# Macaron transformer, attention stage: 256 of 8192 exponentials a channel by a polynomial on VectorE, and q and k of a head on two row blocks

## The chip, the cores and the metric

The kernel runs on one core of one Trainium2 chip. The metric is the device time of one launch in microseconds. The kernel before took 8821.56 us in the median of three runs (8819.5 to 8832.62).

## What is computed

Six layers follow each other on x of shape (4, 1024, 128): a mixture of experts, a state-space layer, the mixture again, a second mixture of experts, an attention, and that mixture again. Each is added to x, most after a layernorm. The change lies in the attention alone, which has 16 heads of 8 columns, and 16 "channels" a head. Cut to what matters:

```
Q, K, V = proj(layernorm(x))                     # (4, 16, 1024, 8)
for wl in range(16):                             # channels
    m = cos(phase_modulators)[wl]                # one number a head
    scores = (Q*m) @ (K*m).T / sqrt(8)
    scores = scores * cos(KERR * scores * scores)   # KERR = 2.7e-12
    acc += softmax(scores) @ V * interference_weights[wl]
out = (acc / 16) @ Wo + bo
```

The kernel takes the inner cosine for 1 when a bound on the scores allows it (both branches are in the program; this input takes the short one, `attention_small`). A channel then differs from another only by the factor cc[h, wl] = m*m/sqrt(8) in front of the same 1024 x 1024 scores.

## The kernel before

**Data.** All of x stays in SBUF. A unit u is one head of one batch, 64 in all. `xs[u]` holds its scores transposed (keys on partitions: 128 x 8 x 1024 fp32, less each query's maximum), two buffers. For each of 16 channels ScalarE makes `p_w = exp(cc * xs)` in one instruction of 8192 columns (L812, two buffers), and TensorE multiplies it by `vt` (the head's 8 value columns and a column of ones, which gives the softmax's sum) into `o`: 32 matmuls of 256 columns (L821), in four column blocks (r = 0 to 3), which the profile counts as 64[...]. VectorE copies `o` to `os` (L829), TensorE transposes it (L842), and every second channel VectorE copies the result into `ot` (L846). After 16 channels `weigh` (L753 to L775) divides by the sums, applies the channels' weights and adds the channels up into `comb`.

**Beside that.** `prepare(u)` makes the scores of a later unit in 16 steps: `maxima` (L721), eight steps that score 128 queries against all keys (two matmuls in `score`, L707, counted as four) and reduce them on VectorE (L726), and, at its end, write the negated maxima by matmul and copy into row 0 of the head's block of `qp` (L734, L741); and `head` (L746), eight steps that score with the maxima in place and copy into `xs` (L750). `group` (L685) projects q and k of HG = 4 heads at a time, each head on its own 32 rows of the 128; `batch` (L647) does a batch's layernorm, transposes and values; `out` (L777) projects a finished batch and adds it to x.

**Order.** TensorE and VectorE run in the written order (manual_schedule, L794). Channel by channel it is: matmuls of `o`; copy `os`; at channel 0, `weigh` of the unit before; pieces of group, batch or out in their channels; one step of `prepare` (channel 15 begins the unit after next); the transposes; at odd channels the copy into `ot`. Each engine takes its queue in order, so an instruction that waits holds up all behind it. ScalarE has only the exponentials: that of channel g+2 writes the `p_w` buffer that the matmuls of channel g read.

Of the kernel before, what the change touches and what calls it, by code (L numbers as in the profile page):

```python
# [26 lines left out]
P = 128  # L27
# [16 lines left out]
PI2_1 = 6.28125  # L44
PI2_2 = 0.0019350051879882812
PI2_3 = 2.0 * math.pi - PI2_1 - PI2_2
RSQRT = 1597463007.0
LN_TINY = -87.33654

# [468 lines left out]
    nc.vector.tensor_tensor(xt, xt, k.bo, op=ALU.add)  # L518


HG = 4
NG = H // HG
QQ = 4
QW = L // QQ


def attention(tc, k):
# [8 lines left out]
    with ExitStack() as ctx:  # L536
# [5 lines left out]
        with (  # L542
            tc.tile_pool(name="at_p", bufs=2) as sb,
            tc.tile_pool(name="at_tr", bufs=2, space=PSUM) as ps_tr,
        ):
            z = half_sine(nc, sb, k.pm, H * WL)
            m = sb.tile([P, H * WL], F32, name="m")
            nc.vector.scalar_tensor_tensor(m, z, -2.0, z, op0=ALU.mult, op1=ALU.mult)
            nc.vector.tensor_scalar(m, m, 1.0, None, op0=ALU.add)
            m_hw = m.rearrange("p (w h) -> p h w", h=H)  # L550
            nc.vector.scalar_tensor_tensor(cc, m_hw, SCALE, m_hw, op0=ALU.mult, op1=ALU.mult)
            nc.vector.tensor_scalar(iw, k.iw, 1.0 / WL, None, op0=ALU.mult)

            pb = ps_tr.tile([1, 2, P], F32, name="pb", tag="tr")
            for j, (w_t, b_t) in enumerate(((k.wq, k.bq), (k.wk, k.bk))):
                w2 = sb.tile([C, C], F32, name="w2")
                nc.vector.tensor_tensor(w2, w_t, w_t, op=ALU.mult)
                pn = ps_tr.tile([P, 1], F32, name="pn", tag="pn")  # L560
                nc.tensor.matmul(pn, w2, k.ones[:, 0:1], start=True, stop=True)
                big = sb.tile([P, 1], F32, name="big")
                nc.scalar.activation(big, pn, AF.Sqrt, scale=1.02 * C)
                ab = sb.tile([P, 1], F32, name="ab")
                nc.vector.scalar_tensor_tensor(
                    ab, b_t, -1.0, b_t, op0=ALU.mult, op1=ALU.max
                )
                nc.vector.tensor_tensor(big, big, ab, op=ALU.add)
                nc.tensor.transpose(pb[:, j, :], big, k.ident)
            both = sb.tile([1, 2], F32, name="both")  # L570
            nc.vector.tensor_reduce(both, pb, AX.X, ALU.max)
            bound = sb.tile([1, 1], F32, name="bound")
            nc.vector.scalar_tensor_tensor(
                bound, both[:, 0:1], SCALE * D, both[:, 1:2], op0=ALU.mult, op1=ALU.mult
            )
            nc.vector.scalar_tensor_tensor(
                bound, bound, KERR, bound, op0=ALU.mult, op1=ALU.mult
            )
            nc.vector.tensor_scalar(bound, bound, 1e-4, None, op0=ALU.is_lt)
            nc.vector.tensor_copy(flag, bound)  # L580
# [13 lines left out]
def attention_small(tc, k, cc, iw):  # L594
# [10 lines left out]
    with (  # L605
# [5 lines left out]
        tc.tile_pool(name="as_o", bufs=1, space=PSUM) as ps_o,  # L611
    ):

        wp, bp = [], []
        for x, w_t in (("q", k.wq), ("k", k.wk)):
            w = one.tile([C, NG, HG, 32], F32, name=f"wp_{x}")
            nc.gpsimd.memset(w, 0.0)
            nc.gpsimd.tensor_copy(
                w[:, :, :, 1 : 1 + D], w_t.rearrange("c (g j d) -> c g j d", j=HG, d=D)
            )  # L620
            wp.append(w)
            b_t = one.tile([P, NG], F32, name=f"bp_{x}")
            nc.gpsimd.memset(b_t, 0.0)
            if x == "k":
                for j in range(HG):
                    nc.gpsimd.memset(b_t[32 * j : 32 * j + 1, :], 1.0)
            for j in range(HG):
                nc.sync.dma_start(
                    out=b_t[32 * j + 1 : 32 * j + 1 + D, :],
                    in_=k.b_dram[x].rearrange("(g j d) -> j d g", j=HG, d=D)[j],  # L630
                )
            bp.append(b_t)
        nm = one.tile([P, GT], F32, name="nm")
        vts = []
        for j in range(2):
            vt = one.tile([P, GT, H, D + 1], F32, name=f"vt{j}")
            nc.gpsimd.memset(vt[:, :, :, D : D + 1], 1.0)
            vts.append(vt)
        ob = []
        for j in range(2):  # L640
            o = ps_o.tile([P, 512], F32, name=f"o{j}", tag=f"o{j}")
            nc.vector.memset(o[:, 0:QW], 0.0)
            ob.append(o)

        xnt, qp, kp, comb, xs = {}, {}, {}, {}, {}

        def batch(b):  # L647

# [5 lines left out]
            for half in range(2):  # L654
                pt = ps_t.tile([P, 4, P], F32, name="pt", tag="tr")
                for i in range(4):
                    t = b * GT + half * 4 + i
                    xn = sb.tile([P, C], F32, name="ln_xn", bufs=4)
                    nc.vector.tensor_scalar(
                        xn,  # L660
                        k.x_sb[:, t, :],
# [23 lines left out]
        def group(n):  # L685

            for w, b_t, x, at in zip(wp, bp, "qk", (qp, kp)):
                at[n] = sb.tile([P, L], F32, name=f"{x}p")
                for half in range(2):
                    pq = ps_t.tile([P, 512], F32, name="pq", tag="tr")  # L690
                    nc.tensor.matmul(
                        pq,
                        w[:, n % NG].rearrange("c j d -> c (j d)"),
                        xnt[n // NG][:, ts(half, 512)],
                        start=True,
                        stop=True,
# [9 lines left out]

        def score(j, a, i, c):  # L707

            row = slice(32 * j, 32 * j + 32)
            s = ps_s.tile([P, L], F32, name="s")  # L710
            for half in range(2):
                nc.tensor.matmul(  # L712
                    s[:, ts(half, 512)],
                    a[row, ts(i, P)],
                    c[row, ts(half, 512)],
                    start=True,
                    stop=True,
                )
            return s

        def maxima(u):  # L721

            n, j = divmod(u, HG)
            row = slice(32 * j, 32 * j + 1)
            for i in range(GT):
                nc.vector.tensor_reduce(  # L726
                    nm[:, i : i + 1], score(j, qp[n], i, kp[n]), AX.X, ALU.max, negate=True
                )
                if i < GT - 1:
                    yield  # L730
            for half in range(2):
                pt = ps_t.tile([P, 4, P], F32, name="pt", tag="tr")
                for i in range(4):
                    nc.tensor.matmul(  # L734
                        pt[row, i, :],
                        nm[:, half * 4 + i : half * 4 + i + 1],
                        k.ident,
                        start=True,
                        stop=True,
                    )  # L740
                nc.vector.tensor_copy(  # L741
                    qp[n][row, ts(half, 512)], pt[row].rearrange("p a b -> p (a b)")
                )
            yield

        def head(u):  # L746
            n, j = divmod(u, HG)
            xs[u] = xp.tile([P, GT, L], F32, name="xs")
            for i in range(GT):
                nc.vector.tensor_copy(xs[u][:, i, :], score(j, kp[n], i, qp[n]))  # L750
                yield

        def weigh(u, ot):  # L753

# [11 lines left out]
            )  # L766

            if h == 0:
                comb[b] = sb.tile([P, 2, QQ, C], F32, name="comb")
            nc.vector.tensor_reduce(  # L770
                comb[b].rearrange("p c r e -> p (c r) e")[:, :, ts(h, D)],
                ot[:, :, :, 0:D].rearrange("p w t d -> p t d w"),
# [21 lines left out]
        with tc.manual_schedule(engines={mybir.EngineType.PE, mybir.EngineType.DVE}):  # L794
            finish(batch(0), group(0), prepare(0))
            ahead = prepare(1)
            next(ahead)
            for u in range(n_heads):
                n, j = divmod(u, HG)
                b, h = divmod(u, H)  # L800

                beside = []
                if j == 2 and n + 1 < B * NG:
                    beside.append((10, 14, group(n + 1)))
                if n % NG == 3 and j == 1 and b + 1 < B:
                    beside.append((4, 9, batch(b + 1)))
                if b > 0 and h == 2:
                    beside.append((2, 10, out(b - 1)))
                ot = sb.tile([P, WL, 2 * QQ, D + 1], F32, name="ot", bufs=1)
                for wl in range(WL):  # L810
                    p_w = xp.tile([P, GT, L], F32, name="p_w")
                    nc.scalar.activation(  # L812
                        p_w.rearrange("p a b -> p (a b)"),
                        xs[u].rearrange("p a b -> p (a b)"),
                        AF.Exp,
                        scale=cc[:, h, wl : wl + 1],
                    )
                    o = ob[wl % 2]
                    for i in range(GT):
                        for r in range(QQ):  # L820
                            nc.tensor.matmul(  # L821
                                o[32 * r : 32 * r + D + 1, 0:QW],
                                vts[b % 2][:, i, h, :],
                                p_w[:, i, ts(r, QW)],
                                start=(i == 0),
                                stop=(i == GT - 1),
                            )
# [7 lines left out]
                    if wl == WL - 1 and u + 2 < n_heads:  # L835
                        finish(ahead)
                        ahead = prepare(u + 2)
                    next(ahead, None)
                    if wl % 2 == 0:
                        pt = ps_t.tile([P, 4, P], F32, name="pt", tag="tr")  # L840
                    for c in range(2):
# [152 lines left out]
def load_attention(nc, pool, k, a):  # L994
# [4 lines left out]
    for x in "vo":  # L999
        get(f"w{x}", [C, C], a[f"L1_attn_W{x}"])  # L1000
        get(f"b{x}", [P, C], a[f"L1_attn_b{x}"].partition_broadcast(P))
    k.b_dram = {x: a[f"L1_attn_b{x}"] for x in "qk"}
    get(
        "pm",
        [P, WL * H],
        a["L1_attn_phase_modulators"].rearrange("w h -> (w h)").partition_broadcast(P),
    )
    get("iw", [P, WL], a["L1_attn_interference_weights"].partition_broadcast(P))


# [93 lines left out]
```

## Time and profile before

| | |
|---|---|
| median of three runs | 8821.56 us |
| the profiled execution | 8833.98 us, span 8832.1 us |
| TensorE busy | 7823.0 us (89%) |
| ScalarE busy | 7665.0 us (87%) |
| VectorE busy | 3262.1 us (37%) |
| GpSimd busy | 608.7 us (7%), nearly all before 1300 us |
| mean granted TensorE clock | 0.918 |
| first exponential of L812 starts | 1424.5 us |
| last exponential of L812 starts | 8654.4 us |

A row of the costliest groups reads: line, engine, operation, tiles written and read, shapes, count, then busy us and mean ns of one, then idle time of the engine just before, and what ended most of it. A row of the timeline reads: start, duration, engine, line, operation, tiles, count; in brackets the engine's idle time before it and who ended it. Busy time on TensorE is modelled from overlapping matmuls, so 89% is not 89% of its peak, and its clock (PEclk) is granted between half and full.

### The profile page before, as it was taken

The page shows a single profiled execution, that of the slowest core. Times are in us where ns is not written, and L with a number is a line of the kernel's source. Part 1 is how long each engine was busy: PE and PEld are TensorE (multiplying, and loading weights), DVE is VectorE, ACT ScalarE, POOL GpSimd, SP SyncE. Part 2 cuts the span into 40 slices and gives each one's busy share as a digit, 9 for nine tenths or more (in the row PEclk, how much of TensorE's full clock was granted, in tenths as well). Part 3 has the DMA queues.
Part 4 walks back from the last instruction along what each step waited for, and adds up shares of the span by engine and source line. Part 5 has one row for each costly group of instructions (what it writes and reads, how often), then busy time and mean ns, then how long its engine had stood idle before and what let it go on. Part 6 is the DMA issues. An engine that isn't in the chain of part 4 may idle for free. (4 is left out here: it accounts for less than half of the span.)

```text
span 8832.1 us, 164134 instructions
## 1 busy us (share of the span) xinstructions
PE 7823.0 (89%) x76474; PEld 3392.0 (38%) x76474; DVE 3262.1 (37%) x5409; ACT 7665.0 (87%) x1746; POOL 608.7 (7%) x579
## 2 busy tenths in 40 slices
PE   8888887999899998989999999999999999899985
PEld 5222253333333333333333333333333333333333
DVE  6777773323333333323233323223333333323222
ACT  3333325999999999999999999999999999999992
POOL 3444430000000000000000000000000000000000
PEclk9777787999999999999999999999999999999996
DMA  0000000000000000000000000000000000000000
GB/s 18 0 0 0 0 6 4 1 1 1 1 1 1 1 1 1 1 1 1 1 1 1 1 1 1 1 1 1 1 1 1 1 1 1 1 1 1 1 1 16
DMA packets 14326, 19.40 MB, mean 2 GB/s; under 512 B 2986, under 2 KB 12722, under 8 KB 13620
## 3 DMA queue, kind: packets, MB, share of 16 engines
q8 instruction: 609, 9.98, 0.5%
q1 hardware_dynamic: 9316, 6.01, 0.2%
q10 hardware_dynamic: 4304, 2.62, 0.1%
q14 instruction: 97, 0.79, 0.0%
HBM read 6.53 MB, written 2.10 MB: 1 GB/s over the span
## 5 line engine op out<-in xcount | busy, mean ns | idle before, releaser
L812 ACT ACTIVATE p_w<-xs,cc 128x8192 f32<-128x8192 f32 x1024 | 7188.6, 7109 | 48.5 <-DVE xs L750 29.1
L821 PE MATMUL o<-p_w,vt 128*9 128x256 f32 x65536 | 4055.1, 403 | 654.3 <-ACT p_w L812 653.4
L821 PEld LDWEIGHTS o<-p_w,vt 128*9 128x9 f32 x65536 | 1809.4, 95 | 2608.2 <-ACT p_w L812 804.3
L829 DVE COPY os<-o 128x256 f32<-128x256 f32 x1024 | 434.9, 425 | 3595.2 <-PE o L821 3595.2
L712 PE MATMUL s<-kp,qp 32*128 32x512 f32 x2048 | 1026.5, 621 | 0.0
L712 PE MATMUL s<-qp,kp 32*128 32x512 f32 x2048 | 1022.1, 619 | 0.0
L750 DVE COPY xs<-s 128x1024 f32<-128x1024 f32 x512 | 627.1, 1225 | 730.4 <-PE s L712 724.3
L726 DVE TENSOR_REDUCE nm<-s 128x1 f32<-128x1024 f32 x512 | 626.2, 1223 | 647.5 <-PE s L712 647.5
L712 PEld LDWEIGHTS s<-qp,kp 32*128 32x128 f32 x2048 | 343.6, 186 | 491.2 <-issue 486.9
L712 PEld LDWEIGHTS s<-kp,qp 32*128 32x128 f32 x2048 | 344.7, 186 | 471.7 <-issue 467.0
L842 PEld LDWEIGHTS pt<-ident,os 128*128 128x128 f32 x2048 | 206.2, 141 | 764.1 <-issue 669.0
L354 PE MATMUL yp<-hm,ident 128*128 128x512 f32 x512 | 388.7, 880 | 99.2 <-POOL hm L353 97.7
L842 PE MATMUL pt<-ident,os 128*128 128x128 f32 x2048 | 450.3, 302 | 19.6 <-DVE os L829 9.6
L336 ACT ACTIVATE da<-delta,neg_a 128x512 f32<-128x512 f32 x256 | 182.7, 721 | 291.9 <-DVE hst L342 291.5
L353 POOL TENSOR_TENSOR hm<-hst,c_sb 128x512 f32<-128x512 f32 x256 | 369.9, 1457 | 166.3 <-ACT c_sb L333 113.3
L178 ACT ACTIVATE r<-hp 128x512 f32<-128x512 f32 x160 | 95.5, 597 | 207.9 <-PE hp L176 185.5
L354 PEld LDWEIGHTS yp<-hm,ident 128*128 128x128 f32 x512 | 110.0, 252 | 348.9 <-POOL hm L353 318.0
L340 DVE TENSOR_TENSOR db<-du,bp 128x512 f32<-128x512 f32 x256 | 164.2, 682 | 152.9 <-PE bp L329 152.0
L333 ACT COPY c_sb<-cp 128x512 f32<-128x512 f32 x128 | 74.8, 585 | 166.1 <-PE cp L331 129.0
L342 DVE TENSOR_TENSOR_SCAN hst<-da,last,db 128x512 f32<-128x512 f32 x128 | 192.0, 1540 | 0.0
L180 POOL TENSOR_TENSOR h<-r 128x512 f32<-128x512 f32 x160 | 164.6, 1047 | 201.7 <-ACT r L178 201.3
L342 DVE TENSOR_TENSOR_SCAN hst<-da,db 128x512 f32<-128x512 f32 x128 | 171.1, 1372 | 5.6 <-POOL hm L353 4.4
(176 smaller groups left out, 3102.8 us busy)
## 6 DMA issues: line engine op xcount, KB each, us to landing
x_sb<-in_L_attn_x_dram ACTq DMA_DIRECT2D x4, 512.0 KB
c_w<-in_L_ffn_w_dram SPq DMA_DIRECT2D x4, 512.0 KB
out_dram<-x_sb SPq DMA_DIRECT2D x4, 512.0 KB
c_w<-in_L_ffn_w_stack_dram SPq DMA_DIRECT2D x1, 512.0 KB
c_w<-in_L_ffn_w_stack_dram ACTq DMA_DIRECT2D x1, 512.0 KB
c_ws<-in_L_ffn_ws_dram SPq DMA_DIRECT2D x2, 128.0 KB
c_w_in<-in_L_attn_W_in_dram SPq DMA_DIRECT2D x1, 256.0 KB
c_w_out<-in_L_attn_W_out_dram SPq DMA_DIRECT2D x1, 128.0 KB
```

Source lines behind the costliest of these rows:

```text
L180: nc.gpsimd.tensor_tensor(h, r, r, op=ALU.mult)
L336: nc.scalar.activation(da, delta[:, c, hc], AF.Exp, scale=neg_a[:, c, n : n + 1])
L342: nc.vector.tensor_tensor_scan(hst, da, db, 0.0 if half == 0 else last[:, c, n : n + 1], op0=ALU.mult, op1=ALU.add,)
L353: nc.gpsimd.tensor_tensor(hm, hst, c_sb, op=ALU.mult)
L354: nc.tensor.matmul(yp[c], k.ident, hm, start=(n == 0), stop=(n == NS - 1))
L712: nc.tensor.matmul(s[:, ts(half, 512)], a[row, ts(i, P)], c[row, ts(half, 512)], start=True, stop=True,)
L726: nc.vector.tensor_reduce(nm[:, i : i + 1], score(j, qp[n], i, kp[n]), AX.X, ALU.max, negate=True)
L750: nc.vector.tensor_copy(xs[u][:, i, :], score(j, kp[n], i, qp[n]))
L812: nc.scalar.activation(p_w.rearrange("p a b -> p (a b)"), xs[u].rearrange("p a b -> p (a b)"), AF.Exp, scale=cc[:, h, wl : wl + 1],)
L821: nc.tensor.matmul(o[32 * r : 32 * r + D + 1, 0:QW], vts[b % 2][:, i, h, :], p_w[:, i, ts(r, QW)], start=(i == 0), stop=(i == GT - 1),)
L829: nc.vector.tensor_copy(os, o[:, 0:QW])
L842: nc.tensor.transpose(pt[:, wl % 2 * 2 + c, :], os[:, ts(c, P)], k.ident)
```

## The change

The first 256 of the 8192 columns of each channel's `p_w` are no longer made by ScalarE. VectorE makes them in nine operations: `split` multiplies by cc/ln 2, rounds to an integer p, forms 2^p by shifting into the exponent (as an integer), and takes the rest r; `power` evaluates a polynomial of degree five in r, short of its leading factor. The factor, EXP2_TOP, is put on the values instead: `vtop`, formed once a head, takes the place of `vt` in the one of 32 matmuls that reads these columns. In VectorE's order, channel g carries `split` of g+3 and `power` of g+2, after the step of `prepare` and ahead of the copy into `ot`; `vtop` stands ahead of the head's channel 0.

A group is 2 heads instead of 4. Each head has its q and k twice, on two blocks of 32 rows; `score` takes its first 512 keys from one block and the other 512 from the other. The maxima go to both blocks, by matmuls of 64 columns and an addition. `group` runs once every two heads, at channels 10 to 13, and forms its padded weights each time on GpSimd; `out` begins at channel 1 of the batch's first head (channel 2 of its third before). `ln_xn` has one buffer instead of four in `batch`, `comb` one instead of two, and the mask `pm` is loaded inside the attention.

```diff
-HG = 4
+HG = 2
+SOFT = 256
...
+        def split(g):
+            u, wl = divmod(g, WL)
+            s, c = xs[u][:, 0, 0:SOFT], cc2[:, u % H, wl : wl + 1]
+            r = sb.tile([P, SOFT], F32, name="x_r")
+            nc.vector.tensor_scalar(r, s, c, -127.0, op0=ALU.mult, op1=ALU.max)
+            p = sb.tile([P, SOFT], F32, name="x_p")
+            nc.vector.tensor_scalar(p, r, ROUND, ROUND, op0=ALU.add, op1=ALU.subtract)
+            e = sb.tile([P, SOFT], I32, name="x_e")
+            nc.vector.tensor_scalar(
+                e, p, float(1 << 23), 127.0 * (1 << 23), op0=ALU.mult, op1=ALU.add
+            )
+            nc.vector.tensor_tensor(r, r, p, op=ALU.subtract)
+            return e, r, p
+
+        def power(g, e, r, p):
+            p_w[g] = xp.tile([P, GT, L], F32, name="p_w")
+            nc.vector.scalar_tensor_tensor(p, r, EXP2[4], r, op0=ALU.add, op1=ALU.mult)
+            for c in EXP2[3], EXP2[2], EXP2[1]:
+                nc.vector.scalar_tensor_tensor(p, p, c, r, op0=ALU.add, op1=ALU.mult)
+            nc.vector.scalar_tensor_tensor(
+                p_w[g][:, 0, 0:SOFT], p, EXP2[0], e.bitcast(F32), op0=ALU.add, op1=ALU.mult
+            )
...
         def score(j, a, i, c):
-            row = slice(32 * j, 32 * j + 32)
             s = ps_s.tile([P, L], F32, name="s")
             for half in range(2):
+                row = slice(64 * j + 32 * half, 64 * j + 32 * half + 32)
                 nc.tensor.matmul(
...
+            nc.vector.tensor_copy(nm[:, :, 32], nm[:, :, 0])
...
-                    xn = sb.tile([P, C], F32, name="ln_xn", bufs=4)
+                    xn = sb.tile([P, C], F32, name="ln_xn", bufs=1)
...
+            power(0, *split(0))
+            power(1, *split(1))
+            parts = split(2)
             for u in range(n_heads):
...
+                vtop = sb.tile([P, D + 1], F32, name="vtop")
+                nc.vector.tensor_scalar(vtop, vts[b % 2][:, 0, h], EXP2_TOP, None, op0=ALU.mult)
                 for wl in range(WL):
-                    p_w = xp.tile([P, GT, L], F32, name="p_w")
+                    g = u * WL + wl
                     nc.scalar.activation(
-                        p_w.rearrange("p a b -> p (a b)"),
-                        xs[u].rearrange("p a b -> p (a b)"),
+                        p_w[g].rearrange("p a b -> p (a b)")[:, SOFT:],
+                        xs[u].rearrange("p a b -> p (a b)")[:, SOFT:],
                         AF.Exp,
                         scale=cc[:, h, wl : wl + 1],
                     )
                     o = ob[wl % 2]
                     for i in range(GT):
                         for r in range(QQ):
+                            soft = i * L + r * QW < SOFT
                             nc.tensor.matmul(
                                 o[32 * r : 32 * r + D + 1, 0:QW],
-                                vts[b % 2][:, i, h, :],
-                                p_w[:, i, ts(r, QW)],
+                                vtop if soft else vts[b % 2][:, i, h, :],
+                                p_w[g][:, i, ts(r, QW)],
...
                     next(ahead, None)
+                    done, parts = parts, split(g + 3) if g + 3 < n_heads * WL else None
+                    if done:
+                        power(g + 2, *done)
```

`vtop` is L860 in the changed kernel.

## The prediction

> **What bounds the kernel now.** I read the page's costliest groups first, then who the exponential waits for, then the timeline of single channels. In the groups, ScalarE's exponential of L812 stands alone:
>
> ```profile
> L812 ACT ACTIVATE p_w<-xs,cc 128x8192 f32<-128x8192 f32 x1024 | 7188.6, 7109 | 48.5 <-DVE xs L750 29.1
> ```
>
> and its tile's view says what its idle time (us, times) ended with:
>
> ```profile
>   DVE xs L750: 29.1, 24
>   PE o L821: 19.0, 10
> ```
>
> 7188.6/1024 = 7.02 us from start to start, and 48.5 us of idle in all. Attention is a ScalarE queue without gaps, so the change can win only by shortening L812, and loses by whatever makes it wait. L812 of channel g+2 needs the TensorE product `o` of channel g (two `p_w` buffers). So look at how late `o` may come, and at what speed TensorE runs it:
>
> ```profile
> 4103.74 5.33 PE L821 MATMUL o<-p_w,vt 128*9 128x256 f32 x64 [0.92 <-ACT p_w L812]
> 4109.00 1.98 PE L712 MATMUL s<-qp,kp 32*128 32x512 f32 x4
> 4109.13 0.42 DVE L829 COPY os<-o 128x256 f32<-128x256 f32 x1 [5.21 <-PE o L821]
> 4110.91 0.44 PE L842 MATMUL pt<-ident,os 128*128 128x128 f32 x2
> 4111.01 1.23 DVE L750 COPY xs<-s 128x1024 f32<-128x1024 f32 x1 [1.46 <-PE s L712]
> ...
> 6630.18 3.64 PE L821 MATMUL o<-p_w,vt 128*9 128x256 f32 x64
> 6638.41 6.06 PE L821 MATMUL o<-p_w,vt 128*9 128x256 f32 x64 [2.31 <-ACT p_w L812]
> ```
>
> The same 64 matmuls take 3.64, 5.33 or 6.06 us. The difference is the granted clock, in the windows around the second and the last:
>
> ```profile
> 4103.74:4107.15 3.41, 3.41 (x36) 1.49 (x40) 0.18 (x1) 3.41 (x1) 0.00 (x0) 0.51 0.03 5
> 6634.80:6638.20 3.40, 1.30 (x5) 0.30 (x3) 1.44 (x2) 3.40 (x1) 0.00 (x0) 0.75 0.00 0
> 6638.20:6641.60 3.40, 3.19 (x32) 1.23 (x36) 0.00 (x0) 3.40 (x2) 0.00 (x0) 0.50 0.00 0
> ```
>
> (columns: us, busy PE, PEld, DVE, ACT, POOL, then PEclk). After a stretch with little `o`, TensorE runs at half clock for 3.4 us, or 6.8. Today this is harmless: exp of g+2 comes due 6.9 us after `o` of g may start.
>
> **The change, part by part.** T = end of an exponential.
>
> *Removed from ScalarE:* 256 of 8192 columns. L336 takes 721 ns for 512 columns, L812 7109 for 8192: (7109-721)/7680 = 0.832 ns a column, 0.213 us a channel, x1024 = **-218 us**. Exponentials then come every 6.80 us.
>
> *Added to VectorE, nine 128x256 operations a channel.* The nearest rows are those of half_sine, same shape, each waiting for the one before:
>
> ```profile
> 1347.93 0.29 DVE L474 TENSOR_SCALAR cs_k<-cs_k 128x256 f32<-128x256 f32 x1
> 1348.26 0.43 DVE L476 SCALAR_TENSOR_TENSOR cs_r<-cs_k,c_pm 128x256 f32<-128x256 f32 x1
> 1348.72 0.42 DVE L477 SCALAR_TENSOR_TENSOR cs_r<-cs_k,cs_r 128x256 f32<-128x256 f32 x1
> ```
>
> Start to start, a dependent tensor_scalar costs 0.33, a dependent scalar_tensor_tensor 0.46; an operation that waits for nothing starts 0.085 before the end of the one before (L103: 0.34 long, 0.257 apart). In order: 0.40 (a per-channel scalar adds 0.07: L268 753 ns, L313 682), 0.33, 0.21, 0.34, four times 0.46, 0.34 = **3.46 us**. In an ordinary channel VectorE copies `os` at T+3.7, reduces or copies scores from T+4.8 to 6.0, does the nine until 9.4, copies `ot` until 9.7; its next `os` comes at 6.8+3.7 = 10.5. It keeps up, with 0.8 us over. Cost there: 0.
>
> *Scores on two row blocks.* Four matmuls one after another take 1.98 us now. Where two heads' blocks meet, the trace has
>
> ```profile
> 1419.79 1.21 PE L712 MATMUL s<-kp,qp 32*128 32x512 f32 x1
> 1419.98 1.05 PE L712 MATMUL s<-qp,kp 32*128 32x512 f32 x1
> 1420.80 1.06 PE L712 MATMUL s<-kp,qp 32*128 32x512 f32 x1
> 1420.83 1.05 PE L712 MATMUL s<-qp,kp 32*128 32x512 f32 x1
> ```
>
> Matmuls of different blocks overlap, and the later head's first even starts ahead of the earlier head's last two. The Trainium skill (TensorE: Matmul & The Clock Gate, Part 3, The mechanism) says that matmuls keep program order. By that rule the pairs 1, 2 of one half and 3, 4 of the other overlap only in the middle: 1.5 us. By the rows the halves run side by side: 1.05 us. I take the rows. The wait of exp(head, 0) for L750 (29.1 us) then goes: **-29**. By the rule it goes too; the 0.45 us would come back below.
>
> *The stall at each head's start.* `vtop` (L860) is formed on VectorE at the head's start, behind everything of channel 15: nine operations and the `ot` copy. It ends at T+9.8 (T = end of exp 15), and TensorE's first matmul of channel 0 waits for it, with all of `o` queued behind. `o(0)` could have started at T+6.85; it starts at T+9.85, after about 4.8 idle us. At full clock it would end at 13.4, and exp(2) is due at 13.5 (6.8+6.8-0.1): nothing lost. But the clock: the nearest row is the 6.06 us after 2.31 idle us, 2.4 us more than 3.64. Bounds: 0 if the clock held, 1.7 for one half-clock window, 3.0 for most of two. The Trainium skill (same page, Part 1: The HAM clock gate) lets the clock fall after a whole idle window of about 3.4 us on a fixed grid; 4.8 idle us hold one in (4.8-3.4)/3.4 = 0.4 of the heads, the 4 us below in 0.2. By the row above a window with 1.30 us of TensorE work was enough, so every head pays. I take the row, 2.4: `o(0)` ends at 15.8, exp(2) starts at 15.95, **2.45 us late**.
>
> Then the weighing (L757 to L770, 4037.66 to 4042.22 = 4.56 us) follows `os(0)`, as before, but now with the nine behind it: `os(1)` starts 0.34+4.56+1.14+3.46 = 9.5 us after `os(0)`, at 25.4, ends at 25.8. TensorE's transposes of channel 1 wait for it, and `o(2)` behind them; TensorE is again idle for some 4 us. Transposes at half clock 0.74, `o(2)` starts at 26.6, takes 3.57+2.4, ends at 32.6. Exp(4) is due at 15.95+13.6 = 29.55: **3.15 us late** (at full clock 0.35, bounds 0.35 and 3.75). Sum 5.6 us x 63 heads = **+353** (bounds 22 and 428; by the skill's rule 63 x (0.35+0.6x2.4) = 113).
>
> *Batches and outputs.* Layernorm through one `ln_xn` buffer: each of eight transposes now makes a round trip (0.34+0.05+0.25+0.2 = 0.85 instead of 0.26 us). With statistics (1352.62 to 1358.08: 5.5 us) some 19 us of VectorE work fall on five channels with about 1.1 us over each; the lead of `o` absorbs 3. I take 10 to 20, say 15, three times; the output projections, now beside the weighing, some 7, three times; today's 19.0 us of waits for `o` are in it: **+46** (20 to 80).
>
> *At nothing:* 16 more groups (4 projections of 1.05 us, 4 copies of 0.75) fall on channels with TensorE at 5.1 of 6.8 us; GpSimd's weight copies (L618: 0.3 us) run on an idle engine and wait only for the group before; `maxima` waits for one more 0.16 us copy. Without that cover they cost up to 16 x 4 x 0.75 = 48 us. The exponential's new wait is for the polynomial of two channels earlier, which `o` of that channel waited for anyway. The mask load moves behind one DMA: 0 to 0.5 us; SP's bias loads follow it.
>
> *Start.* The first head's 16 score steps stand 3.41 us apart at half clock, limited by four matmuls; side by side about 1.9. Saved 25, less 3 for the first polynomials: **-22** (-30 to +5).
>
> Sum: -218-29+353+46-22 = **+130**. The profiled execution took 8833.98 (span 8832.1): 8964. It stands 12 above the median of 8821.56, so I forecast 8821.56+130 = about **8950** for the median.
>
> **Rivals.**
> 1. *The clock holds at the head's start*, or TensorE's idle stretch counts as work. Then the stalls are 22 us: -218-29+22+46-22 = -201, 8620; by the skill's idle window 113, so -110, 8710. For it: at full clock both `o` come almost in time, and most gaps in attention don't trip the clock (some 830 of 1024 `o` in the trace run at 3.6). Against: every stretch as empty as this did. One half-clock window (1.7) each time would give 63 x 3.85 = 243, +20, 8842. It turns faster where an `o` after the gap loses less than 1.6 us. Faster by over 0.2%: 0.14.
> 2. *VectorE's chain is longer*: scores in program order (+0.45) or not side by side (+0.9), or dearer operations. Each 0.45 delays both `o`: 63 x 0.9 = +57; serial scores +113, and the 29 return: 9005 to 9095. 0.22.
> 3. *The exponential doesn't shorten* (its cost not per column): 9170. L336 speaks against: 0.02.
>
> **How the numbers follow.** 0.56 for the forecast (8860 to 9000), 0.22 and 0.02 for the slower ones, 0.14 faster, 0.06 within 0.2% (17.6 us, about what a measurement tells from no change). The range 8820 to 9090 leaves out rival 1's full form, rival 3 and a piece of each side.
>
> **What would show it.** L812 at 6.9 us each with idle near 450 us, its releaser `o`, late at channels 2 and 4 of each head; `o` groups of 5 to 6.5 us at channels 0 and 2; PEld of `o` waiting for `vtop`; the nine operations at 0.29 to 0.43 us; score groups near 1.1 us. Wrong if `o(0)` runs in 3.6 us after the wait, or if VectorE reaches `vtop` before T+7.

## The result and the profile after

The changed kernel took 8931.86 us in the median of four runs (8924.35 to 8940.69), beside 8826.35 (8819.5 to 8832.62) for the kernel before, which had one run more than in the table above: 1.012 times as long, 95% interval 1.0103 to 1.0138. The profiled executions stand 90.4 us apart: 8833.98 before, 8924.35 after.

The row of the exponential on the page of the changed kernel, and two rows of the polynomial:

```profile
L863 ACT ACTIVATE p_w<-xs,cc 128x7936 f32<-128x7936 f32 x1024 | 6979.1, 6898 | 372.5 <-PE o L873 230.6
L789 DVE SCALAR_TENSOR_TENSOR x_p<-x_p,x_r 128x256 f32<-128x256 f32 x3072 | 1306.1, 425 | 105.3
L776 DVE TENSOR_SCALAR x_p<-x_r 128x256 f32<-128x256 f32 x1024 | 301.4, 294 | 35.0
```

ScalarE works 209.5 us less than before and waits 324.0 us longer. Its tile's view lists what the waits end with (us, times):

```profile
  PE o L873: 230.6, 76
  issue: 141.9, 63
```

63 of the waits are put down to "issue", that is, to nothing the profile shows. They are channel 2's. The timeline of head 23 shows what they wait for (T, the end of the last exponential of the head before, is 4049.62):

```profile
4059.05 0.30 DVE L901 COPY ot<-pt 128x144 f32<-128x144 f32 x1
4059.27 0.16 DVE L860 TENSOR_SCALAR vtop<-vt 128x9 f32<-128x9 f32 x1
...
4059.48 0.60 PE L873 MATMUL o<-p_w,vtop 128*9 128x256 f32 x1 [4.75 <-DVE vtop L860]
...
4059.88 5.59 PE L873 MATMUL o<-p_w,vt 128*9 128x256 f32 x59
...
4065.60 13.71 ACT L863 ACTIVATE p_w<-xs,cc 128x7936 f32<-128x7936 f32 x2 [2.38 <-issue]
...
4075.11 0.42 DVE L881 COPY os<-o 128x256 f32<-128x256 f32 x1
...
4075.58 0.69 PE L897 MATMUL pt<-ident,os 128*128 128x128 f32 x2 [4.05 <-DVE os L881]
...
4076.59 5.77 PE L873 MATMUL o<-p_w,vt 128*9 128x256 f32 x59
...
4082.49 6.92 ACT L863 ACTIVATE p_w<-xs,cc 128x7936 f32<-128x7936 f32 x1 [3.18 <-PE o L873]
```

Read downwards: VectorE gets to `vtop` only after channel 15's last copy; TensorE, idle for 4.75 us, then needs 6.0 us for `o(0)`; exp(2) starts 0.13 us after `o(0)` has ended, whatever the bracket says. Then `os(1)` is late, TensorE is idle for 4.05 us, `o(2)` takes 6.2 us, and exp(4) waits. The granted clock during `o(0)` (columns as in the prediction; the column after POOL is PEclk):

```profile
4057.47:4060.89 3.42, 1.41 (x16) 0.61 (x20) 1.79 (x6) 3.42 (x1) 0.00 (x0) 0.50 0.00 0
4060.89:4064.30 3.41, 3.41 (x40) 1.28 (x32) 0.00 (x0) 2.33 (x1) 0.00 (x0) 0.50 0.02 5
4064.30:4067.71 3.41, 3.41 (x48) 1.27 (x41) 2.09 (x4) 2.11 (x1) 0.00 (x0) 1.00 0.00 0
```

Where the time went, from the start-to-start distances of L863 in the trace (median 6.801 us; 7.013 before), as excess over the median:

| us | before | after |
|---|---|---|
| 1023 distances at the median | 7174 | 6957 |
| excess at channel 2 | within 0.5 | 147.7 (all heads but the last) |
| excess at channel 4 | within 0.5 | 175.1 (all heads but the first) |
| excess at all other channels | 55.6 | 64.5 |
| first exponential starts | 1424.5 | 1407.9 |
| from the end of the last one to the end of the span | 170.5 | 162.9 |

-217 + 323 + 9 - 17 - 8 = +90, the difference of the two spans. (323 is channels 2 and 4 together.)

### The profile page after: what moved, and what is told of

The parts are those of the page before. It is cut to its first block, busy times and chain, and to the rows that moved or that the text cites. A ratio compares the mean times of both kernels' runs of the same rounds, so it can differ in the third digit from the quotient of the medians.

```text
span 8922.5 us, 174023 instructions
## 1 busy us (share of the span) xinstructions
PE 7329.0 (82%) x76602; PEld 3158.3 (35%) x76602; DVE 6585.9 (74%) x14818; ACT 7455.7 (84%) x1746; POOL 622.5 (7%) x642
## 5 line engine op out<-in xcount | busy, mean ns | idle before, releaser
L863 ACT ACTIVATE p_w<-xs,cc 128x7936 f32<-128x7936 f32 x1024 | 6979.1, 6898 | 372.5 <-PE o L873 230.6
L789 DVE SCALAR_TENSOR_TENSOR x_p<-x_p,x_r 128x256 f32<-128x256 f32 x3072 | 1306.1, 425 | 105.3
L873 PE MATMUL o<-p_w,vtop 128*9 128x256 f32 x2048 | 671.7, 412 | 307.5 <-DVE vtop L860 307.5
L729 PE MATMUL s<-kp,qp 32*128 32x512 f32 x2048 | 588.5, 651 | 0.7 <-DVE nm L743 0.7
L729 PE MATMUL s<-qp,kp 32*128 32x512 f32 x2048 | 583.1, 646 | 0.0
L790 DVE SCALAR_TENSOR_TENSOR p_w<-x_p,x_e 128x256 f32<-128x256 f32 x1024 | 435.6, 425 | 109.4 <-DVE x_p L789 3.7
L787 DVE SCALAR_TENSOR_TENSOR x_p<-x_r 128x256 f32<-128x256 f32 x1024 | 428.3, 418 | 0.1
L781 DVE TENSOR_TENSOR x_r<-x_r,x_p 128x256 f32<-128x256 f32 x1024 | 428.2, 418 | 0.0
L774 DVE TENSOR_SCALAR x_r<-xs,cc 128x256 f32<-128x256 f32 x1024 | 352.8, 345 | 1.0
L776 DVE TENSOR_SCALAR x_p<-x_r 128x256 f32<-128x256 f32 x1024 | 301.4, 294 | 35.0
```

The source lines that it names most:

```text
L729: nc.tensor.matmul(s[:, ts(half, 512)], a[row, ts(i, P)], c[row, ts(half, 512)], start=True, stop=True,)
L781: nc.vector.tensor_tensor(r, r, p, op=ALU.subtract)
L787: nc.vector.scalar_tensor_tensor(p, r, EXP2[4], r, op0=ALU.add, op1=ALU.mult)
L789: nc.vector.scalar_tensor_tensor(p, p, c, r, op0=ALU.add, op1=ALU.mult)
L790: nc.vector.scalar_tensor_tensor(p_w[g][:, 0, 0:SOFT], p, EXP2[0], e.bitcast(F32), op0=ALU.add, op1=ALU.mult,)
L863: nc.scalar.activation(p_w[g].rearrange("p a b -> p (a b)")[:, SOFT:], xs[u].rearrange("p a b -> p (a b)")[:, SOFT:], AF.Exp, scale=cc[:, ...
```

## The experiments

The theory: `vtop`'s place in VectorE's queue empties TensorE, TensorE's clock halves, and the late `o` holds the exponential; the weighing with nine more operations behind it does it again two channels on. The rivals: the weighing does its part alone; VectorE is overfull around a head's start; the clock has nothing to do with it. All kernels below are edits of the changed one, and the ratios, with their 95% intervals, are to the kernel before, which took 8826.07 to 8827.66 us beside them, so that times of different runs can be compared. "Excess" is that of the table above.

**vtop formed earlier.**

```diff
                     nc.vector.tensor_copy(os, o[:, 0:QW])
+                    if wl == WL - 1 and u + 1 < n_heads:
+                        top = scaled(u + 1)
```

(`scaled` is the multiplication of L860; the head then takes `vtop` from `top`.)

> The scaled values of the next head are formed in channel 15, right behind the copy of os, ahead of that channel's nine polynomial operations. My theory: their place in VectorE's queue starts both stalls. o(0) then starts when exp(0) ends (T+6.85 instead of T+9.85), exp(2) isn't late; os(1) still comes 9.5 us after os(0), at T+20, but o(2) then ends at T+24.8 (27.2 at half clock) and exp(4) is due at T+27.2: its stall goes too. 8932 - 148 - 175 = 8610, up to 40 more where the clock is half. Rival A, the weighing with the nine operations behind it holds channel 4 back by itself: only the 148 us of channel 2 go, 8784. Rival B, VectorE is simply overfull around a head's start: 8880 or more.

Measured: 8644.68 us, 0.9794 (0.978 to 0.9807), 287 below the changed kernel. In the timeline of its head 23:

```profile
3946.33 0.17 DVE L851 TENSOR_SCALAR vtop<-vt 128x9 f32<-128x9 f32 x1
...
3949.10 3.63 PE L880 MATMUL o<-p_w,vt 128*9 128x256 f32 x62 [1.21 <-ACT p_w L870]
...
3962.81 0.44 PE L906 MATMUL pt<-ident,os 128*128 128x128 f32 x2 [2.22 <-DVE os L888]
```

`o(0)` starts when its exponential ends and takes 3.63 us. `os(1)` still comes late, but TensorE now idles 2.22 us over it, not 4.05, and has the time. The excess of the exponentials is 0.3 us at channel 2 and 17.7 at channel 4 (15 of it in the three heads that carry output projections). Without the late `vtop` neither stall comes; that the weighing holds channel 4 by itself (8784) and that VectorE is overfull (8880) are out. `o(2)` was at full clock in 42 of the 63 heads only, and yet in time, so this run alone does not part the lateness from the clock. VectorE does the same work in this kernel.

**TensorE kept busy while it waits.** Nothing is moved; matmuls that nobody reads fill the two idle stretches.

```diff
+                    if u > 0 and wl == 1:
+                        fill(b, o, 32)
...
+                    if wl == WL - 1:
+                        fill(b, o, 36)
```

> No instruction of the changed kernel is moved. TensorE gets matmuls whose product nobody reads, in the two idle stretches: 36 (4.05 us) between channel 15's transposes and o(0), 32 (3.6 us) between channel 1's scores and its transposes; both end before the wait that follows ends. My theory: the stalls are the half clock after idle stretches of 4.75 and 4.05 us. o(0) then takes 3.6 us instead of 4.6 to 6.0 and ends at T+13.45, with exp(2) due at T+13.5; exp(4) is 0.35 late in 63 heads. 8932 - 323 + 22 = 8630. Rival, the clock is lowered for other reasons, or the wait itself costs the time: 8930 or, with the matmuls in the way, more.

Measured: 9038.51 us, 1.024 (1.0226 to 1.0254), which is not what my theory gave; the rival's "or more" allows the number, but not what came of the two stalls. The excess at channel 2 had fallen from 147.7 to 13.4 us, as my theory asks, but that at channel 4 had risen from 175.1 to 390.9. The timeline shows channel 1's filler in one head:

```profile
4111.07 6.43 PE L852 MATMUL o<-vt 128*9 128x256 f32 x64 [4.03 <-DVE os L894]
```

My own edit did this: channel 1's filler wrote the unused half of the `o` that `os(1)` was still to be copied from, waited for that copy, and so filled no gap but lengthened it. The repeat writes to the other `o`:

```diff
-                        fill(b, o, 32)
+                        fill(b, ob[0], 32)
```

> As the filler before, but channel 1's 32 idle matmuls write to the other o buffer, which os(0) has long left, so that they don't wait for os(1) (in the run before they stood in TensorE's queue until os(1) came and then took 6.4 us, and channel 4 lost 391 us). My theory (half clock after idle): channel 4's stall falls to about 0.35 in 63 heads: 9038 - 391 + 22 = 8670, with vtop and the weighing where the change put them. Rival, channel 4's stall is VectorE's lateness alone and full clock doesn't help it: 9038 - 391 + 175 = 8822.

Measured: 8685.23 us, 0.9839 (0.9826 to 0.9853). Head 23 in its timeline:

```profile
3970.05 4.07 PE L852 MATMUL o<-vt 128*9 128x256 f32 x72
...
3974.88 0.38 PE L886 MATMUL o<-p_w,vtop 128*9 128x256 f32 x1 [0.75 <-DVE vtop L873]
...
3975.10 3.41 PE L886 MATMUL o<-p_w,vt 128*9 128x256 f32 x59
...
3988.57 0.44 PE L912 MATMUL pt<-ident,os 128*128 128x128 f32 x2 [0.43 <-DVE os L894]
...
3989.17 3.41 PE L886 MATMUL o<-p_w,vt 128*9 128x256 f32 x59
...
3992.70 6.91 ACT L876 ACTIVATE p_w<-xs,cc 128x7936 f32<-128x7936 f32 x1 [0.34 <-PE o L886]
```

and the clock during `o(0)` and `o(2)`:

```profile
3974.88:3978.52 3.64, 3.64 (x66) 1.74 (x66) 0.00 (x0) 3.64 (x1) 0.00 (x0) 1.00 0.02 5
3989.17:3992.58 3.41, 3.41 (x66) 1.62 (x58) 3.24 (x9) 3.19 (x1) 0.00 (x0) 1.00 0.00 0
```

`vtop` is as late as in the changed kernel, `o(0)` starts as late (9.86 us after T, the middle of 63 heads, in both), and yet `o(0)` and `o(2)` take 3.64 or 3.65 us in all 63 heads, against means of 5.81 and 5.57. Excess: 11.9 us at channel 2, 50.4 at channel 4, half of it in the three heads with output projections. With the wait for `vtop` left as it is and the half clock gone, 261 of the 323 us of excess are gone, and the kernel is 247 us faster for arithmetic that is thrown away. The late `vtop` by itself, at full clock, costs little; the clock after the gap makes the loss.

**No polynomial.** `split`, `power` and `vtop` are left out, and ScalarE makes all 8192 columns.

> The changed kernel without the polynomial: ScalarE makes all 8192 columns, no split, power or vtop. Two row blocks, groups of two heads, one ln_xn buffer and the rest stay. My theory: ScalarE's term returns (1024 x 0.212 = 217), the stalls go (323), and of the batches' 64 us about 45: 8932 + 217 - 323 - 45 = 8780, which is also the kernel before less the waits for xs (29) and the earlier start (17). Rival, the row blocks, the 16 more groups and the single buffer cost up to 48 us that stand hidden in my sum: 8830 or more.

Measured: 8807.13 us, 0.9975 (0.9968 to 0.9983). Its row:

```profile
L859 ACT ACTIVATE p_w<-xs,cc 128x8192 f32<-128x8192 f32 x1024 | 7184.6, 7108 | 42.7 <-PE o L868 34.0
```

It lies midway between the two figures and bears out neither. The waits for xs are down from 29.1 to 8.7 us and the first exponential is 15 us earlier, but 34.0 us of waits for `o` remain, against 19.0: mostly 9 us in each of the three heads with a batch (7.5 to 7.9 of it at channel 9). So the rest of the change is worth about -20 us, not -46, and what it does to the batches costs some 12 us (these three heads had 16.4 us of excess in the kernel before and have 27.9 here) even with VectorE busy for 38% of the span. Which part of that is the single `ln_xn` buffer was not tried by itself. The polynomial alone is then 8932 - 8807 = +125.

**The weighing in two channels.**

```diff
+                    if u > 0 and wl == 1:
+                        add_up(u - 1, last)
```

(`add_up` is the reduction at the end of `weigh`, no longer in it.)

> The last part of the weighing (the adding up, 2.1 us) is moved from channel 0 to channel 1, behind the copy of os; vtop stays where it is. My theory: channel 4's stall comes from os(1) standing behind the whole weighing and the nine operations. os(1) comes 2.1 us earlier, TensorE idles 1.95 instead of 4.05 us: the stall at channel 4 falls from 2.8 to 0.7 at half clock, to nothing at full clock, that of channel 2 stays at 148. 8932 - 175 + (0 to 44) = 8757 to 8800. Rival, the stall at channel 4 is only handed on from channel 2 and its late TensorE work: 8900 to 8930.

Measured: 8771.53 us, 0.9938 (0.9924 to 0.9952), inside the forecast. Channel 2 keeps 137.6 us, channel 4 keeps 17.4: `os(1)` is as early as was worked out (TensorE idles 1.91 us over it in head 23). `o(2)` still ran at half clock for a part in 58 of 63 heads, 5.06 us in the mean, but started early enough for exp(4). So channel 4's stall is not a mere echo of channel 2's, which stays. With the two runs above it takes three things together: a late `o(0)`, the whole weighing ahead of `os(1)`, and the half clock; without any one of them it is nearly gone (17.7, 17.4 and 50.4 us of 175.1). Channel 2's stall takes the late `vtop` and the half clock.

**Both moves.** The two edits above together.

> Both moves: the scaled values in channel 15 behind os, and the adding up of the weighing in channel 1. My theory: with the values ahead, channels 2 and 4 have no stall left that the second move could take; it may only take the 0.4 us at channel 9 of some heads (15 us in all). 8645 - (0 to 15) = 8630 to 8645. Rival, the two moves' gains add up (287 and 160): 8485.

Measured: 8646.04 us, 0.9796 (0.9783 to 0.9809): no different from `vtop` ahead alone. Gains at one stall don't add. The 0.4 us at channel 9 didn't go either. By the timeline they belong to channel 6, where the end of `maxima` puts sixteen matmuls and two additions between `os(6)` and its transposes, and `o(7)`, which exp(9) waits for, stands behind; no run tried this by itself.

**One row block for the scores.**

```diff
-                row = slice(64 * j + 32 * half, 64 * j + 32 * half + 32)
+                row = slice(64 * j, 64 * j + 32)
```

> The changed kernel with all score matmuls of a head on its first block of 32 rows (the second block is written and not read). A step's four matmuls then take 1.98 us instead of 1.13. By the prediction's second rival each of the two late o is 0.9 us later in 63 heads, 113 us, and the waits for xs return, 29 us: 8932 + 142 = 9074. Against it: longer scores leave TensorE less idle before the late o, so that the clock may hold more often, 8930 or less; or VectorE, which waits for each step's scores in every channel, falls behind everywhere, 9200 or more.

Measured: 9071.76 us, 1.0281 (1.0267 to 1.0295). The two steps that matter in its timeline:

```profile
4142.70 1.98 PE L729 MATMUL s<-kp,qp 32*128 32x512 f32 x4
4147.01 0.69 PE L897 MATMUL pt<-ident,os 128*128 128x128 f32 x2 [2.33 <-DVE os L881]
```

The total is the 9074 that was worked out, but not by its terms. Channels 2 and 4 grew by 36 us together, not 113; channel 0 by 34 (the view lists 26.3 us of waits for xs); the start is 28 us later; some 53 us fall on channels 6 to 11, two thirds of it in the six heads with batches or output projections. (These are parts of the profiled execution, 161 us longer than that of the changed kernel; the medians are 140 apart.) At channel 1 the longer scores left TensorE idle for 2.33 us instead of 4.05, since `os(1)` came no later after `o(0)` than before (9.61 us after its end, in both): what they cost there was idle time already. The agreement of the sum is chance, and the run bears out only what the second row block saves as a whole, 140 us.

**A version that beats both.** `vtop` ahead and the weighing in two channels, with four `ln_xn` buffers, the batch's statistics and layernorm spread over channels 3 to 13, and the output projections over eight channels from 2 to 15.

> Both moves of the run beside it, and the remaining waits thinned: four ln_xn buffers instead of one, a batch's statistics and layernorm in eleven channels instead of five, the output projections spread over channels 2 to 15. With the values ahead the stalls at channels 4, 8, 9 and 11 were 13 us a batch and 12 us an output, three of each. I expect two thirds of these 75 us and the 15 of channel 9 to go: 8645 - 50 - 15 = 8580. Rival, the pieces cost the same wherever they stand, since each makes TensorE wait for VectorE: 8630.

Measured: 8569.45 us, 0.9716 (0.9702 to 0.9729).

```profile
L892 ACT ACTIVATE p_w<-xs,cc 128x7936 f32<-128x7936 f32 x1024 | 6971.3, 6900 | 21.1 <-ACT p_w L892 15.5
```

Idle is 21 us in all: ScalarE is the bound again, as it was before the change, with 217 us less to do. The stalls of batches and outputs went nearly all (excess 29 us, of which 22 at channel 9), more than I had expected. The buffers and the two spreads were changed together, so what each is worth stays open; that these waits must be paid whatever one does is out.

## Why the prediction was right

The direction, the place and the mechanism held, and 8950 lay 18 us over the measured 8932. Some of that closeness is luck: +130 was forecast, from an execution 12 us above its median, and the change measured +106 by the medians run side by side and +90 by the profiled executions. By its steps:

- *The exponential shortens by 0.213 us a channel, -218.* Measured: 7108 less 6898 ns, 0.212 us a distance, -217. 0.832 ns a column, from two rows of other sizes, held at a third size.
- *Nine operations cost 3.46 us, nothing in an ordinary channel.* They run at 0.29 to 0.43 us each. From the start of the first to the start of the copy behind them it is 3.49 us in head 23 (4055.56 to 4059.05). The ordinary channels 3, 5, 7 and 10 to 15 have an excess of 7 us together.
- *The stall at each head's start.* In head 23, as times after T: `vtop` ends at 9.81 (predicted 9.8), `o(0)` ends at 15.85 (15.8), exp(2) starts at 15.98 (15.95), `os(1)` at 25.49 (25.4), `o(2)` at 26.58 (26.6) and ends at 32.74 (32.6), exp(4) starts at 32.87 (32.7). Head 23 is a dear one, though. Over the 63 heads the excess is 2.32 us at channel 2, against 2.45, and 2.78 at channel 4, against 3.15, 0.13 of which is the output projections'. **Mis-sized term:** the half clock's 2.4 us for each `o`. It was taken from one row, for every head; the mean was 5.81 - 3.64 = 2.17 and 5.57 - 3.64 = 1.93, 44 us less in 63 heads. The row was a dear one: of the 28 `o` in the trace of before that had waited 2.2 to 2.4 us, 19 took 5.33, four 6.05 to 6.51, two about 5.1, and three 3.64. With 8 us of the output projections and 2 of head 0 in it, +353 became +323.
- *Whether the clock falls without a whole idle window.* The Trainium skill (TensorE: Matmul & The Clock Gate, Part 1: The HAM clock gate) has it fall after a whole idle window of about 3.4 us. By this the sum was 113 us; 323 were measured. The windows at channels 1 and 2 of head 24:

```profile
4183.76:4187.18 3.42, 1.40 (x12) 0.30 (x4) 3.32 (x8) 3.42 (x2) 0.00 (x0) 1.00 0.00 0
4187.18:4190.59 3.41, 1.39 (x10) 0.58 (x14) 3.20 (x8) 3.41 (x1) 0.00 (x0) 0.50 0.00 0
4190.59:4194.00 3.41, 3.41 (x36) 1.29 (x32) 3.16 (x9) 2.35 (x1) 0.00 (x0) 0.50 0.02 5
```

  The idle stretch of 4.04 us lies across a boundary; neither window that it touches is idle, each holds 1.4 us of TensorE work, and each is followed by one at half clock. A window of the grid was wholly idle in 41 heads ahead of `o(0)` and in 20 ahead of `o(2)`; `o` ran at half clock for a part in all 63, at both channels. So "every head pays" was right. The reason that the prediction gave, a window with 1.30 us of TensorE work, was not: its window 6634.80:6638.20 lies across a boundary, as its clock of 0.75 shows. Cut at the boundaries:

```profile
6633.12:6636.53 3.41, 2.98 (x22) 0.97 (x10) 1.19 (x2) 3.41 (x1) 0.00 (x0) 1.00 0.00 0
6636.53:6639.95 3.42, 1.54 (x16) 0.60 (x20) 0.68 (x2) 3.42 (x2) 0.00 (x0) 0.50 0.00 0
```

  The window before the half clock held 2.98 us of TensorE work, of which 0.70 was `o`. The prediction's other words, "a stretch with little `o`", fit better (see the last section).
- *Scores side by side, 1.05 us a step.* 1.13 by the timeline, 1.98 with one block. So TensorE does not run matmuls of two row blocks one behind the other, while an instruction that waits does hold up what stands behind it, as with the 4.75 us before `o(0)`. That the exponential no longer waits for xs, -29, holds in the changed kernel (its view lists no such wait); without the polynomial 8.7 of the 29 stayed.
- *Batches and outputs, +46, with the -29 in the same channels.* Together +17 predicted; +9 measured at the channels other than 2 and 4, and 8 more of the outputs at channel 4. Right as a sum; the three batches cost 41 us, for which 45 were taken, and the three outputs 30, for which 21 were taken. Some 12 us of the batches' came without the polynomial too.
- *Start, -22.* -17 at the first exponential. Another 8 us came after the last one, which the sum didn't have: 2.9 of them because the last `o`, 6.51 us at half clock before, took 3.63.

Of the rivals, the first (clock holds, 8620) is what the filler made: 8685, with the kernel's own instructions in the same order. So the clock decides the sign, as the prediction said; its turning point, 1.6 us lost by each `o`, no run tried. The second and the third are out by the rows: a score step took 1.13 us, the nine operations 3.49, the exponential 6.90.

## What to carry to other kernels

Before adding work to an engine that has time left, look for the small instruction that another engine waits for once a round: what counts is what stands ahead of it in its queue, not the free share. Put such an instruction where its inputs are ready, in another round if need be. And when a gap is tolerable at full speed, ask what the engine behind it runs at after the gap: here the same late `vtop` cost 62 us of excess with the clock held (22 by the prediction) and 323 without.

## What was not expected of the hardware

- Busy time is not what keeps the clock up. In the kernel before, a window with 3.25 us of TensorE work (scores, transposes and the maxima's matmuls, no `o`) was followed by one at half clock; in the changed kernel, a window with 1.44 us, all of it `o`, was followed by one at full clock:

```profile
4759.20:4762.61 3.41, 3.25 (x12) 1.55 (x13) 1.77 (x6) 3.41 (x2) 0.00 (x0) 1.00 0.00 0
4762.61:4766.03 3.42, 3.42 (x20) 1.77 (x22) 2.18 (x3) 3.42 (x1) 0.00 (x0) 0.50 0.00 0
...
4781.10:4784.51 3.41, 1.44 (x26) 0.51 (x18) 3.23 (x10) 3.41 (x1) 0.00 (x0) 1.00 0.00 0
4784.51:4787.92 3.41, 0.34 (x2) 0.18 (x2) 2.64 (x7) 3.41 (x2) 0.00 (x0) 1.00 0.00 0
```

  From 1450 to 8600 us, no window at full clock with more than 1.29 us of `o` before, or 1.14 after, was followed by half clock; many with less were not either. What exactly is counted these runs don't show.
- A half-clock window with 2.37 us of TensorE work in it (4074.54 to 4077.95) was followed by another at half clock, one with 2.86 us (4173.52 to 4176.94) by one at full clock.
- The clock changes on a fixed grid of 3.41 us (every change in both traces within 0.01 us of it), and the stall follows that grid: the idle stretch ahead of `o(2)` was 4.0 to 4.1 us long in 58 of the 63 heads, yet the stalls at channels 2 and 4 were 2.96 and 1.82 us in head 22, 2.47 and 3.27 in head 23, 1.51 and 2.78 in head 24, and so on in threes through most of the heads.
- The length of an idle stretch alone doesn't tell: 2.22 us at channel 1 (`vtop` ahead, head 23) left `o(2)` at full clock, as in 42 of the 63 heads of that version, and 1.91 us at the same place (weighing in two channels, head 23) cost it a window. After the 4 us and more of the changed kernel it was slow in all 63.
